# Causal attention in a decoder layer: query tiles of odd number with their quarters reversed, masked quarter products left out of every diagonal block, and the softmax sums' reciprocals turned on VectorE

## The chip, the cores and the metric

The kernel runs as one program on one core of a Trainium2 chip. The metric is the time of one execution on the device, in microseconds (us). A core has five engines that run their own instruction lists and wait for each other by semaphores: TensorE (PE in the profile; PEld is its loading of weights), VectorE (DVE), ScalarE (ACT), GpSimd (POOL) and SyncE (SP), which here issues most of the DMA transfers.

## The reference

A decoder layer on x (2 x 1024 tokens x 256 channels) with a context of 2 x 77 tokens, all in float32:

```python
x = _layernorm(x + self_attention(x))       # causal, 16 heads of 64, rotary positions on q and k
x = _layernorm(x + cross_attention(x, ctx)) # 16 heads of 64, 77 keys
x = _layernorm(x + routed_ffn(x))           # half of the tokens, hidden width 1024, exact gelu
```

The change lies in the self-attention, which for each batch and head is:

```python
sim = einsum('bid,bjd->bij', rope(x @ Wq), rope(x @ Wk)) * 64**-0.5
sim = where(tril, sim, -inf)
out = einsum('bij,bjd->bid', softmax(sim), x @ Wv)
```

A query i has no product with keys j > i: their weights are zero after the softmax.

## The kernel before

Self-attention takes the first 555 us or so of the execution, cross-attention and the feed-forward network the rest. Heads are worked two at a time: a `Pair` is one batch and two heads (their 128 channels), 16 pairs in all. Tokens are cut into 8 tiles of 128, and each tile into 4 quarters of 32.

For a pair the steps are, with the letters that the hand-written order uses:

- `P`, `E`: q, k and v are projected on TensorE (L257, L292) and copied out of PSUM by ScalarE (L265, L301).
- `d`, `c`, `s`, `a`: rotary positions, for half of the tokens at a time (0 or 1) and for k and q in one 128x1024 instruction each: two DMAs swap neighbouring rows (`swap`), GpSimd multiplies by the cosine (`cosine`, L277) and the swapped copy by the sine (L280), and adds both into the tile `kq` (`rotated`, L284). VectorE does this for half 0 of pair 0.
- `S`, `T`, `X`: scores of query tiles in five groups, (3,1,0), (4,2), (5), (6), (7), on TensorE (L331), each for keys up to the query tile's own; VectorE adds the tile `fence`, which holds the causal mask for the diagonal block in its last 128 columns and zeros before them, and takes the least (L344); ScalarE takes the exponential and its sum over keys (L352).
- `R`: VectorE turns the weights within 32x32 squares (L361) into `p_t`. There the partitions of quarter r hold the queries of quarter r's squares with keys down the partitions, so the product with the values is made of small matmuls on 32 rows and 64 columns of TensorE: row group r for quarter r of the queries, column group j for the head.
- `V0` to `V7` (`output`, L399): V*n* takes key tile n, for each of its quarters k, each head j and each row group r one matmul into `po[r]`, over the queries of the same quarter r in all query tiles from n on: 256, 224, ... 32 columns. For n < 7 all of them are made, also those of the diagonal block whose quarter of keys lies wholly after the quarter of queries (k > r); their weights are zeros. For n = 7 those are left out.
- `O`: ScalarE copies the four `po` out, quarter r to columns r*32 and on of each tile (L413); for the last pair VectorE multiplies while it copies (L419).
- `Q`, `I`, `D`, `B`, `M`, `W`: the sums are turned by a TensorE transpose into a PSUM tile `pr` (`sums_row`, L369), VectorE takes the reciprocal, 16x128, (L373), one DMA writes it to DRAM, 16 rows of 512 bytes (`flat`), two DMAs read it back spread over 64 partitions each (`along`), GpSimd multiplies (L422), and a DMA stores the pair's output.
- `w`, `l`: the values go to DRAM and come back in four copies, one for each row group, two of them issued by ScalarE.

After the 16 pairs the outputs are projected tile by tile, 8 matmuls each (`Closing.project`, L466), and normed.

All engines of this part follow an order written by hand. The list `steps` gives one period, in which steps of different pairs are interleaved; on TensorE it reads: S0 V0 V1 S1 V2 V3 V4 S2 V5 V6 V7 S3 Q Pk1 Pv0 S4 Pq1 Pq0 Pk0 Pv4. `opening` and `ending` give the first and the last pairs one by one. The DMAs of SP leave in the same order (`begin`), and the first of them after V1 and after V7 waits for that step's last matmul (`gate`). A PSUM ring of four buffers serves projections, `pr` and the four `po` in turn. The list `pieces` says, for each pair, how many matmuls are cut into smaller ones (`split`), which adds instructions.

The biases b2 and the router's row w_r of the feed-forward network are loaded early, after the stores of pairs 3 and 4.

Of the kernel before, what the change touches and what calls it, by code (L numbers as in the profile page):

```python
# [22 lines left out]
NT = T // P  # L23
# [11 lines left out]
def decoder_layer(  # L35
# [45 lines left out]
    causal = const.tile([P, P], F32)  # L81
    make_causal_mask(nc, causal, MASKED)
# [37 lines left out]
    b2 = const.tile([P, C], F32)  # L120
    b_r = const.tile([P, 1], F32)
    b1 = const.tile([P, NF], F32)
    w_r = const.tile([P, C], F32)
# [11 lines left out]
    with (  # L135
# [9 lines left out]
        fence = s1.tile([P, T], F32, name="fence")  # L145
        G.memset(fence[:, : T - P], 0.0)
        G.tensor_copy(fence[:, T - P :], causal)
        wo = s1.tile([P, NP, C], F32, name="wo")

        p_t = s1.tile([P, (NT + 1) * NT, P], F32, name="pT")  # L150
        attn_d = [dram.tile([NP, P, T], F32, tag="attn", name="attn_d") for _ in range(B)]
# [3 lines left out]
        def load(t, src):  # L155
            return lambda: nc.sync.dma_start(t, src)


        def load_next(h):
            if h == 0:  # L160
# [10 lines left out]
            3: [load(b2, L0_ffn_b2.partition_broadcast(P)), load(b_r, L0_ffn_b_r.partition_broadcast(P))],  # L171
            4: [
                load(w_r, L0_ffn_w_r.rearrange("c o -> (o c)").partition_broadcast(P)),
# [60 lines left out]

        class Pair:
# [39 lines left out]

            def cosine(self, n, E=G):
                E.tensor_tensor(self.kq[:, :, n * NB : (n + 1) * NB], self.raw[n], self.twice(cos, n), ALU.mult)  # L277
# [4 lines left out]
            def rotated(self, n, E=G):  # L282
                dst = self.kq[:, :, n * NB : (n + 1) * NB]
                E.tensor_tensor(dst, dst, self.turned[n], ALU.add)  # L284
# [54 lines left out]
            def least(self, g, j):  # L339
# [3 lines left out]
                for i, (t, span) in enumerate(self.spans[g]):  # L343
                    V.tensor_tensor_reduce(  # L344
                        p[:, span], self.ps[j][:, span], fence[:, T - (t + 1) * P :],
# [21 lines left out]
            def sums_row(self):  # L367
                self.pr = ring.tile([2 * NT, P], F32, tag="t", name="pr_sums")
                TE.transpose(self.pr, self.sums.rearrange("p j t -> p (j t)"), ident)  # L369

            def inverse(self):
                self.inv = small.tile([2 * NT, P], F32, tag="inv", name="inv", bufs=2)
                V.reciprocal(self.inv, self.pr)  # L373

            def flat(self):
                self.inv_d = dram.tile([2, NT * P], F32, tag="inv", name="inv_d")
                begin(self.inv_d.rearrange("j (t q) -> (j t) q", q=P), self.inv)
# [10 lines left out]
            def output(self, n):  # L388
                if n == 0:
                    self.po = [ring.tile([P, NT, R32], F32, tag="t", name="po_self") for _ in range(4)]  # L390
                for k in range(4):
                    for j in range(2):
                        first = (NT * n + n, NT * (n + 1) + n)[j]
                        step = (1, NT)[j]
                        last = first + (NT - 1 - n) * step + 1

# [861 lines left out]
```

## Time and profile before

| | |
|---|---|
| median of 3 runs | 796.13 us (793.79 to 797.62) |
| the profiled execution | 793.43 us |
| its span in the profile | 791.7 us, granted TensorE clock 0.997 |
| PE busy | 765.8 us, 97% of the span |
| PEld busy | 611.0 us, 77% |
| DVE busy | 556.8 us, 70% |
| ACT busy | 388.6 us, 49% |
| POOL busy | 369.4 us, 47% |

The profile is one execution. Its time as a run is 793.43 us; the span of its instructions is 1.7 us shorter. A group of the profile is given as line, engine, operation, written tile <- read tiles, shape and count, then busy time and mean duration, then the idle time of the engine just before those instructions and what ended it. "issue" there is idle time for which the profile shows nothing that was waited for. The chain of waits is followed backwards from the last instruction; each piece of it has its start, its length and its line. One pair's period in the middle of the self-attention is about 30 us long.

### The profile page before, as it was taken

The page shows a single profiled execution, that of the slowest core. Times are in us where ns is not written, and L with a number is a line of the kernel's source. Part 1 is how long each engine was busy: PE and PEld are TensorE (multiplying, and loading weights), DVE is VectorE, ACT ScalarE, POOL GpSimd, SP SyncE. Part 2 cuts the span into 40 slices and gives each one's busy share as a digit, 9 for nine tenths or more (in the row PEclk, how much of TensorE's full clock was granted, in tenths as well). Part 3 has the DMA queues.
Part 4 walks back from the last instruction along what each step waited for, and adds up shares of the span by engine and source line. Part 5 has one row for each costly group of instructions (what it writes and reads, how often), then busy time and mean ns, then how long its engine had stood idle before and what let it go on. Part 6 is the DMA issues. An engine that isn't in the chain of part 4 may idle for free.

```text
span 791.7 us, 26856 instructions
## 1 busy us (share of the span) xinstructions
PE 765.8 (97%) x11320; PEld 611.0 (77%) x11320; DVE 556.8 (70%) x1295; ACT 388.6 (49%) x1249; POOL 369.4 (47%) x264
## 2 busy tenths in 40 slices
PE   8998999999999999999999998989999999999996
PEld 5565788888888788888887877678967888777755
DVE  2578679769669669677787787915576678758773
ACT  2555456556566466554555554400565666552130
POOL 3633554554554554573654744124023332371665
PEclk9999999999999999999999999999999999999998
DMA  5456377477477476576573655766069888861131
GB/s 199 129 154 178 117 220 191 168 205 188 141 198 196 150 235 180 164 207 179 165 209 104 193 150 175 176 189 224 2 185 246 210 196 216 200 159 54 54 107 53
DMA packets 141412, 131.96 MB, mean 167 GB/s; under 512 B 79554, under 2 KB 117996, under 8 KB 141292
## 3 DMA queue, kind: packets, MB, share of 16 engines
q1 hardware_dynamic: 133132, 100.09, 46.5%
q10 hardware_dynamic: 6624, 25.96, 11.0%
q0 software_dynamic: 1536, 4.20, 1.5%
q8 instruction: 89, 1.46, 0.8%
q14 instruction: 31, 0.25, 0.1%
HBM read 81.68 MB, written 31.76 MB: 143 GB/s over the span
## 4 chain that ended last, share of the span: by engine, by line
PE 76%; DVE 8%; POOL 7%; issue 4%; DMA 2%; SPq 1%; ACT 1%; POOLq 0%; DVEq 0%; ACTq 0%
PE po_self L399 18%; PE ps_scores L331 16%; PE pp_kq L257 13%; PE pp_v L292 7%; PE po_proj L466 6%; PE po_cross L1044 4%; PE ps_cross L974 4%; PE pp_h L907 2%; POOL e_all L1002 2%; POOL comp L842 2%; PE po_ffn L922 2%; DVE reach L812 2%; DVE pT L361 1%; DMA turned<-raw 1%; DVE p L344 1%
## 5 line engine op out<-in xcount | busy, mean ns | idle before, releaser
L352 ACT ACTIVATE p<-p,neg 128x768 f32<-128x768 f32 (+7 forms) x256 | 196.3, 768 | 162.1 <-DVE neg L344 160.1
L344 DVE CUSTOM_DVE_ANT_0 p<-ps_scores,fence 128x512 f32<-128x512 f32 (+7 forms) x256 | 179.4, 750 | 103.4 <-PE ps_scores L331 103.0
L361 DVE STREAM_TRANSPOSE pT<-p 128x512 f32<-128x512 f32 (+7 forms) x256 | 175.7, 740 | 6.2 <-PE po_self L399 3.0
L399 PE MATMUL po_self<-pT,v 32*64 32x256 f32 (+6 forms) x7808 | 156.7, 295 | 11.4 <-issue 8.7
L399 PEld LDWEIGHTS po_self<-pT,v 32*64 32x64 f32 x7808 | 136.9, 130 | 35.6 <-issue 24.9
L331 PE MATMUL ps_scores<-kq 64*128 64x256 f32 (+3 forms) x1060 | 149.7, 411 | 1.5 <-POOL kq L284 0.8
L331 PEld LDWEIGHTS ps_scores<-kq 64*128 64x128 f32 x1060 | 94.4, 186 | 42.0 <-issue 27.1
L257 PE MATMUL pp_kq<-xT,w_pair 128*128 128x256 f32 (+2 forms) x524 | 118.6, 379 | 1.1 <-ACT xT L192 0.7
L280 POOL TENSOR_TENSOR turned<-turned,sin 128x1024 f32<-128x1024 f32 x31 | 73.3, 2363 | 94.4 <-DMA turned<-raw 81.5
L277 POOL TENSOR_TENSOR kq<-raw,cos 128x1024 f32<-128x1024 f32 x31 | 73.6, 2374 | 85.5 <-ACT raw L265 85.5
L257 PEld LDWEIGHTS pp_kq<-xT,w_pair 128*128 128x128 f32 x524 | 88.3, 190 | 23.9 <-issue 11.2
L993 ACT ACTIVATE e_all<-ps_cross,top 128x77 f32<-128x77 f32 x256 | 79.1, 340 | 53.2 <-DVE top L985 51.2
L1002 POOL TENSOR_TENSOR e_all<-e_all,inv 128x616 f32<-128x616 f32 x32 | 38.8, 1217 | 91.1 <-DVE inv L1000 91.0
L109 POOL TENSOR_TENSOR rs<-ve,neg_half 128x1 f32<-128x1 f32 x48 | 26.8, 561 | 107.9 <-DVE ve L107 107.7
L284 POOL TENSOR_TENSOR kq<-kq,turned 128x1024 f32<-128x1024 f32 x31 | 73.6, 2373 | 1.4
L1044 PE MATMUL po_cross<-packed,pT 128*128 128x256 f32 (+1 forms) x320 | 72.3, 380 | 0.3 <-DMA packed<-vo_d 0.3
L974 PE MATMUL ps_cross<-wqk,x1T 128*128 128x308 f32 x256 | 69.9, 425 | 0.3 <-ACT e_all L993 0.3
L1044 PEld LDWEIGHTS po_cross<-packed,pT 128*128 128x128 f32 (+1 forms) x320 | 60.0, 190 | 9.4 <-issue 0.7
L292 PEld LDWEIGHTS pp_v<-w_pair,xT 128*128 128x128 f32 x512 | 61.1, 192 | 4.0 <-issue 2.5
L292 PE MATMUL pp_v<-w_pair,xT 128*128 128x128 f32 x512 | 62.2, 275 | 0.0
L974 PEld LDWEIGHTS ps_cross<-wqk,x1T 128*128 128x128 f32 x256 | 47.2, 190 | 17.5 <-ACT e_all L993 1.4
L993 ACT ACTIVATION_READ_ACCUMULATOR e_all<-ps_cross,top 128x1 f32 x256 | 56.6, 221 | 0.0
(128 smaller groups left out, 787.2 us busy)
## 6 DMA issues: line engine op xcount, KB each, us to landing
turned<-raw SPq DMA_DIRECT2D x64, 256.0 KB, 5.0
v<-v_d ACTq DMA_DIRECT2D x32, 512.0 KB, 10.1
v<-v_d SPq DMA_DIRECT2D x32, 512.0 KB, 11.1
part_d<-part ACTq DMA_DIRECT2D x14, 640.0 KB, 4.4
pT<-part_d SPq DMA_DIRECT2D x56, 160.0 KB, 4.1
v_d<-v SPq DMA_DIRECT2D x16, 512.0 KB, 4.8
over<-inv_d SPq DMA_DIRECT2D x32, 256.0 KB, 4.7
attn_d<-out_pair SPq DMA_DIRECT2D x14, 512.0 KB, 4.2
```

Source lines behind the costliest of these rows:

```text
L257: TE.matmul(pp[:, cols], self.w[:, c, "kq".index(of), :], x_ts[self.b, n][:, c, cols], start=(c == 0), stop=(c == NC - 1),)
L277: E.tensor_tensor(self.kq[:, :, n * NB : (n + 1) * NB], self.raw[n], self.twice(cos, n), ALU.mult)
L284: E.tensor_tensor(dst, dst, self.turned[n], ALU.add)
L292: TE.matmul(pv[:, i, :], x_ts[self.b, 2 * n // NT][:, c, toks], self.w[:, c, 2, :], start=(c == 0), stop=(c == NC - 1),)
L331: TE.matmul(self.ps[j][:, cols], self.kq[rows, 1, t * P : (t + 1) * P], self.kq[rows, 0, cols.start - at : cols.stop - at], start=True, st ...
L344: V.tensor_tensor_reduce(p[:, span], self.ps[j][:, span], fence[:, T - (t + 1) * P :], -SCALE, -MASKED, ALU.add, ALU.min, neg[:, i : i + 1],)
L352: A.activation(p[:, span], p[:, span], AF.Exp, bias=neg[:, i : i + 1], scale=-1.0, accum_out=self.sums[:, j, t : t + 1],)
L361: V.transpose(p_t[:, first : first + t * step + 1 : step, :], self.p[g, j][:, span].rearrange("p (n k) -> p n k", k=P),)
L399: ins = TE.matmul(self.po[r][j * D : (j + 1) * D, n:, :], self.v4[rows, NT * k + n, j * D : (j + 1) * D], p_t[rows, first:last:step, k * R ...
L974: TE.matmul(ps[:, g, : Q * S], self.x_t[:, c, :], wqk[:, c, self.b, h : h + Q, :].rearrange("p h s -> p (h s)"), start=(c == 0), stop=(c = ...
L993: A.activation(self.e[:, hh * HH + h, :], sc[:, g, q, :], AF.Exp, bias=top[:, g, q : q + 1], accum_out=sums[:, h : h + 1],)
L1044: TE.matmul(po, self.p_t[:w, k, :], of[:w, k, :], start=(k == 0), stop=(k == NK - 1))
```

## The change

- The q half of `kq` is written with a new order of columns: in query tiles of odd number the four quarters stand in reverse order. Row group r then holds quarter r of even tiles and quarter 3-r of odd ones. `cosine` and `rotated` therefore become three instructions each: k, the even tiles of q, the odd tiles of q.
- A second fence holds the mask for the odd tiles' order of rows.
- `output` takes key tiles in twos. For each (key tile a, key quarter k) a row group whose quarter of queries in tile a lies wholly before the keys begins at tile a+1, so its matmul is 32 columns narrower (for a = 7 it is left out). The number of matmuls of a pair stays 244. Steps V0 to V7 keep their places in the order, but an even step now holds (m,0), (m+1,0), (m,1), (m+1,3) and the odd one (m,2), (m+1,2), (m,3), (m+1,1), with m the even key tile.
- The copies out of `po` put the quarters back.
- `sums_row` no longer uses TensorE and PSUM: VectorE takes the reciprocal of the sums as they lie (128x16, into a 128x32 tile), and `inverse` turns that tile within 32x32 squares on VectorE. `flat` becomes four DMAs, each of 16 partitions with 128 bytes.
- b2 and w_r are loaded at the start of the cross-attention, in a pool there.

```diff
-    causal = const.tile([P, P], F32)
-    make_causal_mask(nc, causal, MASKED)
-    b2 = const.tile([P, C], F32)
-    w_r = const.tile([P, C], F32)
...
-        fence = s1.tile([P, T], F32, name="fence")
-        G.memset(fence[:, : T - P], 0.0)
-        G.tensor_copy(fence[:, T - P :], causal)
+        fences = [s1.tile([P, T], F32, name=f"fence_{i}") for i in range(2)]
+        make_causal_mask(nc, fences[0][:, T - P :], MASKED)
+        G.memset(fences[0][:, : T - P], 0.0)
+        G.memset(fences[1], 0.0)
+        for r in range(4):
+            rows = fences[1][r * R32 : (r + 1) * R32, T - P :]
+            G.affine_select(
+                out=rows, in_=rows, compare_op=ALU.is_ge, fill=MASKED, base=(3 - r) * R32,
+                pattern=[[-1, P]], channel_multiplier=1,
+            )
...
+        invs = [s1.tile([P, R32], F32, name=f"inv_{i}") for i in range(2)]
+        for t in invs:
+            G.memset(t, 1.0)
...
-            3: [load(b2, L0_ffn_b2.partition_broadcast(P)), load(b_r, L0_ffn_b_r.partition_broadcast(P))],
+            3: [load(b_r, L0_ffn_b_r.partition_broadcast(P))],
             4: [
-                load(w_r, L0_ffn_w_r.rearrange("c o -> (o c)").partition_broadcast(P)),
...
+        def blocks(t):
+            return t.rearrange("p (t two r q) -> p t two r q", two=2, r=4, q=R32)
+        def tiles_of(t, odd):
+            return t if odd is None else blocks(t)[:, :, odd, :, :]
+        def turned_rows(t, r):
+            return t.rearrange("p t q -> p (t q)").rearrange("p (t b q) -> p t b q", b=8, q=R32)[:, :, r : 8 - r : 7 - 2 * r, :]
...
+            def parts(self, n):
+                k, q = (self.kq[:, i, n * NB : (n + 1) * NB] for i in range(2))
+                return [(k, 0, None)] + [(blocks(q)[:, :, i, :: 1 - 2 * i, :], 1, i) for i in range(2)]
             def cosine(self, n, E=G):
-                E.tensor_tensor(self.kq[:, :, n * NB : (n + 1) * NB], self.raw[n], self.twice(cos, n), ALU.mult)
+                for dst, i, odd in self.parts(n):
+                    E.tensor_tensor(
+                        dst, tiles_of(self.raw[n][:, i, :], odd), tiles_of(cos[:, n * NB : (n + 1) * NB], odd), ALU.mult
+                    )
             def rotated(self, n, E=G):
-                dst = self.kq[:, :, n * NB : (n + 1) * NB]
-                E.tensor_tensor(dst, dst, self.turned[n], ALU.add)
+                for dst, i, odd in self.parts(n):
+                    E.tensor_tensor(dst, dst, tiles_of(self.turned[n][:, i, :], odd), ALU.add)
...
-                        p[:, span], self.ps[j][:, span], fence[:, T - (t + 1) * P :],
+                        p[:, span], self.ps[j][:, span], fences[t % 2][:, T - (t + 1) * P :],
...
             def sums_row(self):
-                self.pr = ring.tile([2 * NT, P], F32, tag="t", name="pr_sums")
-                TE.transpose(self.pr, self.sums.rearrange("p j t -> p (j t)"), ident)
+                V.reciprocal(invs[self.n % 2][:, : 2 * NT], self.sums.rearrange("p j t -> p (j t)"))
             def inverse(self):
-                self.inv = small.tile([2 * NT, P], F32, tag="inv", name="inv", bufs=2)
-                V.reciprocal(self.inv, self.pr)
+                self.inv = small.tile([P, R32], F32, tag="inv", name="inv", bufs=2)
+                V.transpose(self.inv, invs[self.n % 2])
             def flat(self):
                 self.inv_d = dram.tile([2, NT * P], F32, tag="inv", name="inv_d")
-                begin(self.inv_d.rearrange("j (t q) -> (j t) q", q=P), self.inv)
+                dst = self.inv_d.rearrange("j (t b q) -> (j t) b q", b=8, q=R32)
+                for r in range(4):
+                    begin(dst[:, r : 8 - r : 7 - 2 * r, :], self.inv[r * R32 : r * R32 + 2 * NT, :])
...
-                for k in range(4):
+                m = n - n % 2
+                for a, k in [((m, 0), (m + 1, 0), (m, 1), (m + 1, 3)), ((m, 2), (m + 1, 2), (m, 3), (m + 1, 1))][n % 2]:
                     for j in range(2):
-                        first = (NT * n + n, NT * (n + 1) + n)[j]
-                        step = (1, NT)[j]
-                        last = first + (NT - 1 - n) * step + 1
-
-                        for r in range(k if n == NT - 1 else 0, 4):
+                        for r in range(4):
+                            t = a if (r, 3 - r)[a % 2] >= k else a + 1
+                            if t == NT:
+                                continue
+                            first = (NT * a + t, NT * (t + 1) + a)[j]
+                            step = (1, NT)[j]
                             rows = slice(r * R32, (r + 1) * R32)
                             ins = TE.matmul(
-                                self.po[r][j * D : (j + 1) * D, n:, :],
-                                self.v4[rows, NT * k + n, j * D : (j + 1) * D],
-                                p_t[rows, first:last:step, k * R32 : (k + 1) * R32],
-                                start=(n == 0 and k == 0), stop=(n == NT - 1 and k == r),
+                                self.po[r][j * D : (j + 1) * D, t:, :],
+                                self.v4[rows, NT * k + a, j * D : (j + 1) * D],
+                                p_t[rows, first : first + (NT - 1 - t) * step + 1 : step, k * R32 : (k + 1) * R32],
+                                start=(a == 0 and k == 0), stop=(m == NT - 2 and (a, k) == ((NT - 1, 1), (NT - 2, 3))[r == 3]),
                             )
...
-                A.copy(self.out[:, :, r * R32 : (r + 1) * R32], self.po[r])
+                A.copy(turned_rows(self.out, r), self.po[r].rearrange("p (t two) q -> p t two q", two=2))
...
+    b2 = c1.tile([P, C], F32, name="b2")
+    w_r = c1.tile([P, C], F32, name="w_r")
+    nc.sync.dma_start(w_r, L0_ffn_w_r.rearrange("c o -> (o c)").partition_broadcast(P))
+    nc.sync.dma_start(b2, L0_ffn_b2.partition_broadcast(P))
```

## The prediction

> **What bounds the kernel now.** First the page: busy shares, then the chain that ended last.
>
> ```profile
> span 791.7 us, 26856 instructions
> PE 76%; DVE 8%; POOL 7%; issue 4%; DMA 2%; SPq 1%; ACT 1%; POOLq 0%; DVEq 0%; ACTq 0%
> ...
> L399 PE MATMUL po_self<-pT,v 32*64 32x256 f32 (+6 forms) x7808 | 156.7, 295 | 11.4 <-issue 8.7
> L399 PEld LDWEIGHTS po_self<-pT,v 32*64 32x64 f32 x7808 | 136.9, 130 | 35.6 <-issue 24.9
> ```
>
> TensorE ends the execution, and L399, the line that is narrowed, is its largest part. Shares are averages, so I took the chain in order of time. One pair, the seventh:
>
> ```profile
> 229.46 1.72 PE ps_scores L331 x16
> 231.17 3.42 PE po_self L399 x128
> 234.60 1.93 PE ps_scores L331 x12
> 236.53 3.80 PE po_self L399 x192
> 240.33 1.49 PE ps_scores L331 x8
> 241.82 2.29 PE po_self L399 x126
> 244.11 1.72 PE ps_scores L331 x16
> 245.83 0.21 PE pr_sums L369
> ```
>
> Piece follows piece without a gap: from about 80 to 476 us (pairs 1 to 13) nothing but TensorE is on the path. VectorE is busy 22.64 of the 30.23 us of this period, GpSimd 16.80. What TensorE saves here is saved, until another wait appears. A stage view says which stretches can shrink: V0 and V1 take 3.43 us for 128 records, V2 to V4 3.80 for 192, V5 to V7 2.29 for 168.
>
> The third view, TensorE's own row by time, shows the one cost in L399 that is not matmul work (the eighth pair):
>
> ```profile
> 270.85 1.15 PE L399 MATMUL po_self<-pT,v 32*64 32x96 f32 x73
> 272.95 1.36 PE L399 MATMUL po_self<-pT,v 32*64 32x64 f32 x95 [0.95 <-issue]
> ```
>
> A stop of 0.95 us with nothing waited for. The queue of instruction packets explains it: 89 packets of 16 KB for some 22,900 instructions of TensorE, so 256 each, and the stops come where the count of instructions passes one remainder by 256, 2.4 to 2.9 us after a packet began to move. In pairs 2 to 13 they add up to about 4.7 us.
>
> **The change, part by part.** The sum is made against the profiled execution, 793.43 us; the median is 796.13, 2.7 above it, and I carry the difference over.
>
> *Narrower matmuls.* The records of V0 start in bursts of eight, one for each 32x64 tile of the array, 216 ns apart at 256 columns; then 189 at 224, 162 at 192, 135, 109, 82 at 96: 27 ns for 32 columns. A matmul has two records (7808 for 16 pairs of 244). In two steps of V, three times in turn some row groups and then the others are 32 columns narrower, so each row group loses 3 x 2 x 27 = 0.16 us. This is worth something only if a row group can run ahead of the rest. The records say yes: when the last pair's first four matmuls start alone at 509.95, the second record of the first comes 267 ns after its first, and the first records of the three others have started in between, out of the program's order.
>
> V0 and V1: -0.16. V2 to V4: -0.16 for key tiles 2 and 3, -0.16 because V4 now holds narrower work (870 to 710 ns), and V5 keeps its 0.66. V6 and V7: their bursts are already at 57 ns, near eight starts of 6.7 ns, so nothing. That is 0.48 us for a pair, 6.2 for the 13 pairs on the pure chain. Pair 0 stands between instruction stops and pair 15's V6 waits 2.57 us for instructions: 0.2 each. Pair 14 isn't TensorE's: 0. Sum -6.6; bounds 0 (no running ahead) and 16 x 0.64 = -10.2 (V6 and V7 gain too).
>
> The Trainium skill, "TensorE: Matmul & The Clock Gate", part 3, "The mechanism", says that matmuls start and end strictly in the program's order. By that rule a step lasts as long as its widest row group, no step is narrow in all four, and this term would be 0. The starts at 509.95 contradict it, so the sum goes by the trace.
>
> *No pr_sums.* From the last score to the next projection the switch costs 93 ns beyond the stream, with pr_sums between 209: -0.116 us, 14 times on the path, -1.6. Bounds 0 and 16 x 0.21 = -3.4.
>
> *Instruction stops.* The number of instructions stays, less two or three for each pair, so the packet boundaries move later by 3 instructions at pair 1 and some 30 at pair 13; `pieces` is unchanged. The stop in V6 follows S2 by a fixed time and moves with it. The one in V4 comes sooner by what V2 and V3 save: half of the pairs have margin there, half have none (their stops are 0 to 0.55). I take +0.12 for each of 13 pairs, +1.5. Bounds: -4.7 (all stops vanish) and +6.2 (all of the gain is waited away).
>
> *GpSimd.* A 128x1024 becomes 128x512 and two of 128x256.
>
> ```profile
> L284 POOL TENSOR_TENSOR kq<-kq,turned 128x1024 f32<-128x1024 f32 x31 | 73.6, 2373 | 1.4
> L459 POOL TENSOR_TENSOR xb<-x,bo 128x256 f32<-128x256 f32 x16 | 11.0, 699 | 0.0
> ...
> 290.38 2.39 POOL L284 TENSOR_TENSOR kq<-kq,turned 128x1024 f32<-128x1024 f32 x1
> 293.99 2.00 PE L331 MATMUL ps_scores<-kq 64*128 64x256 f32 x16
> ```
>
> By these rows 512 columns take 1257 ns and the three 2655, 0.28 more, for `cosine` and `rotated` each: 1.1 us for a pair, on an engine that idles 13. The closest reader is S1, which waits for half 1's `rotated`: it ends at 292.77, S1 starts at 293.99, 1.2 us later. S1 will come 0.16 earlier, and in the built program it waits for the first two parts only (1957 ns), so the cover of the odd part is S2, 5 us on. Cost 0. No row shows runs of 32 backwards; if they doubled a part (1400), S1's two would end 0.28 later, still covered. On VectorE (pair 0) the parts cost 0.3 more each; `rotated` ends at 16.77 and S0 starts at 19.09: 0.
>
> *VectorE.* The reciprocal of 16x128 takes 933 ns and of 128x8 191; so 128x16 some 240, and the 32-column turn some 171 (270 at 128, 1.03 ns a column): 0.41 for 0.93. Hidden in the middle; at the end it is on the chain:
>
> ```profile
> 506.13 0.86 DVE inv L373
> 506.99 0.97 DVE pT L361
> 507.96 0.83 DVE inv L373
> 508.79 2.23 DVE pT L361 x2
> ```
>
> Both stand before the last pair's V0: -0.9. Bounds 0 and -1.7. The fences' extra work on GpSimd (some 2.5 us) is done by 7 us, and VectorE's first read is at 21: 0.
>
> *SP.* `flat` issues four DMAs for one, +1.2 us at the 0.33 to 0.54 us of its rows. In the middle SP idles from 287.3 until V1 opens the next DMA at 294, and `along` comes after that: 0, though the two added waits on the value copies hold up the weights for three pairs later and the store, which nobody needs soon. At the end there is no cover:
>
> ```profile
> 507.02 0.33 SPq L208 DMA_DIRECT2D inv_d<-inv  x1
> 511.79 1.58 SPq L208 DMA_DIRECT2D over<-inv_d  x2
> ...
> 514.10 0.49 SPq L208 DMA_DIRECT2D inv_d<-inv  x1
> 520.13 1.09 SPq L208 DMA_DIRECT2D over<-inv_d  x2
> ```
>
> `along` waits for the write to land (4.8 and 6.0 us), and pair 15's stands behind pair 14's: 2 x 1.2 = 2.4 us later. VectorE multiplies at 526.28 to 527.70, and TensorE uses the result at 529.45: 1.75 us of cover, which TensorE's earlier V7 uses up. I take +1.5; bounds 0 and +4. The loads of b2 and w_r wait for exponentials of the last pairs and fall into SP's idle time from 540 to 577.7: 0.
>
> Sum: -6.6 - 1.6 + 1.5 - 0.9 + 1.5 = -6.1. 793.43 becomes 787.3, the median 790.0.
>
> **Rivals.** What this measurement can tell from no change is 0.5%, 4.0 us.
>
> *The instructions don't come faster.* Stops take the place of the gain. For it: half of the pairs already stop in V, and 256 instructions pass there in 3.4 to 4 us. Against it: a stop moves with S2, and pairs such as the seventh have none. At +6.2 instead of +1.5 the sum is -1.4: 794.7.
>
> *Row groups march in step.* First term 0, no added stops: -1.6 - 0.9 + 1.5 = -1.0: 795.1. Against it: the records at 509.95.
>
> *Backward runs of 32 are dear on GpSimd* (the other side). S1 starts late once its two parts pass 2.37 + 0.84 + 0.2 = 3.4 us, so once a 256-column part takes 2.1 us, three times the 699 ns row. At five times, 3.5 us, S1 is 1.35 late in 13 pairs, +17.5, and the sum +11: 807. It decides from about 2.9 us a part, where the sum passes 4. Against it: the normalising product on 128x616 with a repeated operand costs less per column than the plain one (1217 ns).
>
> *More than forecast:* V6 and V7 gain and stops vanish: -12, 784.
>
> **How the numbers follow.** Forecast 0.64, more 0.06, instructions 0.14, in step 0.06, GpSimd or another slower case 0.10. The forecast's own range, stops and end taken at their bounds one at a time, is 785 to 793; a tenth of it falls short of 0.5%. Faster 0.70, same 0.20, slower 0.10. For eight in ten the range runs from 785 to 797, over both cases without a change.
>
> **What would show it.** V0-V1 near 3.27 us and V2-V4 near 3.25 in a pair without a stop, V5-V7 still 2.29; matmul records of L399 unchanged at 7808; no pr_sums; stops in L399 in more pairs but not longer than 1 us; GpSimd's even part done before S1; `along` of pair 15 later after its write. Wrong it would be if V0-V1 stays at 3.43, if score matmuls wait for kq, or if the po_proj after V7 waits several us for out_pair.

## The result, and the profile after

The changed kernel took 820.82 us (median of 4 runs, 819.41 to 825.33); the kernel before took 795.63 beside it. The ratio is 1.0326, with a 95% interval of 1.0279 to 1.0373. The forecast was 790.0 with a range of 785 to 797: wrong in size and in sign. The profiled execution after took 820.90 us, its span 819.1, 27.4 longer than the span before.

First the page of the kernel after: the span, the chain's shares, and the two groups of the narrowed line (the last number of a group is the engine's idle time just before its instructions, and what ended it).

```profile
span 819.1 us, 27080 instructions
...
PE 80%; DVE 6%; issue 6%; POOL 5%; DMA 2%; ACT 1%; POOLq 0%; ACTq 0%; SPq 0%; DVEq 0%
...
L426 PE MATMUL po_self<-pT,v 32*64 32x224 f32 (+7 forms) x7808 | 154.9, 293 | 32.5 <-issue 30.7
L426 PEld LDWEIGHTS po_self<-pT,v 32*64 32x64 f32 x7808 | 138.7, 134 | 56.4 <-issue 49.7
```

L426 is the old L399. Its busy time fell a little, from 156.7 to 154.9, but TensorE stood still before it for 32.5 us, not 11.4, and "issue" says that nothing the profile shows was waited for. The chain in order of time shows where, in pair 7 (start, length, what):

```profile
266.50 3.27 PE po_self L426 x116
269.76 1.93 PE ps_scores L355 x12
271.69 2.83 PE po_self L426 x124
274.52 2.34 issue
276.87 0.94 PE po_self L426 x29
277.81 2.86 PE ps_scores L355 x8
280.67 2.17 PE po_self L426 x114
282.85 1.72 PE ps_scores L355 x16
```

V0 and V1 take 3.27 us, exactly the forecast. Then, inside V4, TensorE stops for 2.34 us. This is an instruction stop, of the kind that the prediction knew, but it is there in every pair from 2 to 13, 0.72 to 2.69 us long. After it the eight score matmuls, 1.49 us in other pairs, take 2.86. The same stretch by windows shows why (stretch, its length, busy time of PE, PEld, DVE, ACT and POOL with counts, granted TensorE clock, DMA share, GB/s):

```profile
271.62:274.53 2.91, 2.90 (x155) 2.73 (x154) 2.81 (x9) 0.66 (x1) 2.03 (x3) 1.00 0.96 276
274.53:276.87 2.34, 0.00 (x1) 0.00 (x0) 2.02 (x6) 2.27 (x8) 1.19 (x1) 1.00 0.14 32
276.87:277.74 0.87, 0.87 (x39) 0.75 (x38) 0.00 (x0) 0.00 (x0) 0.69 (x1) 0.70 0.00 0
277.74:280.60 2.86, 2.86 (x11) 1.18 (x8) 0.00 (x0) 0.00 (x0) 1.66 (x1) 0.50 0.03 9
```

Two things are to be seen. The DMA engines are 96% busy just ahead of the stop, and the clock granted to TensorE is halved after it.

I added up TensorE's records of both profiles by line, each piece counted to the start of the next. The matmuls with the values take 19.4 us more: 21.4 more of stops, 2.0 less of all else. The same score, projection and output-projection matmuls take 3.1, 1.2 and 3.2 us more; the granted clock is 0.5 to 0.7 for some microseconds after five of the stops, and its mean is 0.982 against 0.997. The transposes of the sums save 2.0. That is 24.9 of the 27.4 us; 1.7 more lie in the feed-forward network's first product, and the rest is in pieces below 1 us. Scores run for 10.3 us at half clock, output projections for 4.5 and the first product for 3.4; no projection of q and k does. Their 1.2 us are mostly the first projection of a pair, which takes 0.10 us longer where it now follows the scores directly.

### The profile page after: what moved, and what is told of

Same layout as the page of the kernel before. It is cut to its first block, busy times and chain, and to the rows that moved or that the text cites. A ratio compares the mean times of both kernels' runs of the same rounds, so it can differ in the third digit from the quotient of the medians.

```text
span 819.1 us, 27080 instructions
## 1 busy us (share of the span) xinstructions
PE 771.7 (94%) x11304; PEld 617.5 (75%) x11304; DVE 547.2 (67%) x1315; ACT 390.1 (48%) x1249; POOL 388.4 (47%) x394
## 4 chain that ended last, share of the span: by engine, by line
PE 80%; DVE 6%; issue 6%; POOL 5%; DMA 2%; ACT 1%; POOLq 0%; ACTq 0%; SPq 0%; DVEq 0%
PE po_self L426 18%; PE ps_scores L355 17%; PE pp_kq L273 14%; PE pp_v L316 7%; PE po_proj L495 6%; PE ps_cross L1007 4%; PE po_cross L1077 4%; PE pp_h L940 3%; POOL e_all L1035 2%; POOL comp L875 2%; PE po_ffn L955 2%; DVE reach L845 1%; DMA v<-v_d 1%; DVE part L1042 1%; DVE pT L385 1%
## 5 line engine op out<-in xcount | busy, mean ns | idle before, releaser
L426 PE MATMUL po_self<-pT,v 32*64 32x224 f32 (+7 forms) x7808 | 154.9, 293 | 32.5 <-issue 30.7
L426 PEld LDWEIGHTS po_self<-pT,v 32*64 32x64 f32 x7808 | 138.7, 134 | 56.4 <-issue 49.7
L355 PE MATMUL ps_scores<-kq 64*128 64x256 f32 (+3 forms) x1060 | 153.0, 421 | 1.3 <-DVE pT L385 1.3
L299 POOL TENSOR_TENSOR kq<-raw,cos 128x256 f32<-128x256 f32 (+1 forms) x93 | 82.3, 915 | 101.6 <-ACT raw L281 101.6
L308 POOL TENSOR_TENSOR kq<-kq,turned 128x256 f32<-128x256 f32 (+1 forms) x93 | 82.3, 915 | 1.4
```

The costliest lines, as they stand in the source:

```text
L299: E.tensor_tensor(dst, tiles_of(self.raw[n][:, i, :], odd), tiles_of(cos[:, n * NB : (n + 1) * NB], odd), ALU.mult)
L308: E.tensor_tensor(dst, dst, tiles_of(self.turned[n][:, i, :], odd), ALU.add)
L355: TE.matmul(self.ps[j][:, cols], self.kq[rows, 1, t * P : (t + 1) * P], self.kq[rows, 0, cols.start - at : cols.stop - at], start=True, st ...
L426: ins = TE.matmul(self.po[r][j * D : (j + 1) * D, t:, :], self.v4[rows, NT * k + a, j * D : (j + 1) * D], p_t[rows, first : first + (NT - ...
```

## The experiments

The DMAs that load the swapped rows (`turned`) and the spread reciprocals (`over`) wait for V1's last matmul. Their packets start 1.4 us after V1's end and keep the DMA engines busy until 6 to 7 us after it. Times are counted here from the start of S1, which is 0.07 us ahead of V1's modelled end in most pairs and up to 0.7 us behind it where S1 waits; so those packets start about 1.5 us after S1's start. For each pair I took from the trace where the boundary of 256 TensorE instructions falls within V2 (the stops stand exactly 256 instructions later, in V4), and when the packet that starts as TensorE gets there (the "request") begins to move. Pairs 2 to 13 (the stops in sums over these pairs):

```
kernel               boundary in V2   request after S1's start  stops, us: V2-V4  V5-V7   ratio to before
                     (instructions)   (us)
before               27 to 40          1.06 to 2.85                  0.9    3.1
after                34 to 61          2.87 to 4.84                 22.1    3.0    1.0326
retuned              26 to 34          1.47 to 4.87                  9.1    6.4    1.0055
shifted              27 to 65          2.35 to 4.68                 16.9    4.6    1.0260
threeparts           27 to 40          1.02 to 2.67                  0.7    4.5    1.0005
retuned_wide         26 to 34          1.05 to 4.26                  6.3    3.8    1.0036
recip                34 to 62          2.21 to 4.58                 18.9    5.7    1.0392
gate4                34 to 61          2.61 to 3.55                  9.6    7.1    1.0089
gate4_before         27 to 40          1.04 to 2.06                  0.0    0.6    0.9914
retuned_flat         26 to 34          1.23 to 2.98                  2.7    2.9    1.0082
gate4_retuned        26 to 34          1.19 to 3.43                  4.0    2.2    0.9907
gate4_retuned_flat   26 to 34          1.10 to 2.73                  0.7    0.3    0.9961
gate4_retuned_wide   26 to 34          1.11 to 3.76                  2.9    0.6    0.9930
gate4_shifted        27 to 65          1.49 to 3.33                  4.8    6.8    1.0084
gate4_late           26 to 34          1.14 to 2.04                  0.03   1.6    0.9818
gate4_late_wide      26 to 34          1.14 to 2.01                  0.0    0.2    0.9883
```

The stops are those of one profiled execution, the ratios are of several. Ratios are compared rather than times, since the kernel before had medians of 795.6 to 801.5 us beside the different sets.

### Is it the boundary, GpSimd, or the narrow steps?

Three theories were on record. P: the boundary lies too late. G: GpSimd's three parts release S1 later. N: the narrower steps pass 256 instructions too quickly for any packet.

`retuned`, the kernel after with other numbers in `pieces`:

```diff
-        pieces = [2, 1, 13, 13, 11, 10, 11, 12, 13, 12, 8, 9, 8, 8, 9, 0]
+        pieces = [2, 1, 14, 13, 12, 11, 10, 12, 13, 12, 9, 9, 8, 9, 9, 1]
```

> The kernel after, with six numbers of pieces changed, so that the boundaries of 256 TensorE instructions lie 26 to 34 instructions into V2 in pairs 2 to 13, as before (27 to 40), and not 34 to 62. Theory P (place of the boundary): the packet is asked for when the queue enters the block, in the kernel after too late to slip in ahead of the transfers that V1's end releases. Then the stops in V2 to V4 of pairs 2 to 13 fall from 22.0 us to under 5 and the time is 786 to 794 us. Theory G (GpSimd's three parts end later, S1 is released later, the queue can't run ahead): only pairs 10 to 13 gain, where the parts end 2.6 us before S1, 7 us in all: 811 to 815. Theory N (the narrower steps pass 256 instructions too quickly for any packet): stops remain in all pairs, 815 or more.

Measured: 806.83 us, 1.0055 (1.0019 to 1.0092). Four fifths of the loss is gone, with the narrow steps and GpSimd's parts as they were, so N falls. (Seven numbers of `pieces` differ.) But 9.1 us of stops are left in V2 to V4, where P expected under 5, and the time misses P's 786 to 794.

`shifted`, the kernel before, its `pieces` changed the other way:

```diff
-        pieces = [2, 1, 13, 13, 11, 10, 11, 12, 13, 12, 8, 9, 8, 8, 9, 0]
+        pieces = [2, 1, 13, 13, 10, 10, 10, 12, 13, 12, 7, 9, 8, 7, 9, 0]
```

> The kernel before, with pieces changed the other way: in pairs 4 to 13 the boundary lies 46 to 66 instructions into V2, as in the kernel after. Nothing else differs. Theory P: stops of 1 to 2.7 us in V4 of these ten pairs, 12 to 24 us in all, time 808 to 822. Theories G and N: 794 to 800, since GpSimd's instructions and the steps' widths are those of before.

Measured: 822.12 us, 1.0260 (1.0211 to 1.0310). The narrowed line's group in this kernel:

```profile
L399 PE MATMUL po_self<-pT,v 32*64 32x256 f32 (+6 forms) x7808 | 163.8, 302 | 32.2 <-issue 29.9 <-DVE pT L361 1.9
```

Idle 32.2 us where the kernel before has 11.4, and nothing of the change is in it: a few matmuls were left uncut. P holds.

`threeparts`, the kernel before with GpSimd's instructions in three parts (`parts` gives k, the even tiles of q and the odd ones, in their old order of columns):

```diff
...
-                E.tensor_tensor(self.kq[:, :, n * NB : (n + 1) * NB], self.raw[n], self.twice(cos, n), ALU.mult)
+                for dst, i, of in self.parts(n):
+                    E.tensor_tensor(dst, of(self.raw[n][:, i, :]), of(cos[:, n * NB : (n + 1) * NB]), ALU.mult)
...
-                E.tensor_tensor(dst, dst, self.turned[n], ALU.add)
+                for dst, i, of in self.parts(n):
+                    E.tensor_tensor(dst, dst, of(self.turned[n][:, i, :]), ALU.add)
```

> The kernel before, with cosine and rotated made in three instructions each (k, even tiles of q, odd tiles of q) with the quarters left in order. Theory G: S1's release comes 0.3 to 0.6 us later against V1's end, packets are late in pairs 2 to 9, time 804 to 815. Theory P: the boundaries are where they were, time 794 to 800.

Measured: 801.00 us, 1.0005 (0.9966 to 1.0043). The parts cost nothing; G falls.

`retuned_wide`, the kernel `retuned` without the narrowing:

```diff
-                            t = a if (r, 3 - r)[a % 2] >= k else a + 1
+                            t = a if a < NT - 1 or (r, 3 - r)[a % 2] >= k else a + 1
```

> The kernel retuned, but with the masked products made again as wide as before in key tiles 0 to 6 (those of key tile 7 stay left out); the number of instructions is the same, so the boundaries stay. It gives the price of the narrower products by itself. If the row groups run ahead of each other as forecast: 3.43 us again for V0 and V1, 3.56 for V2 to V4, and 5 to 7 us more than retuned. If they march in step: the same as retuned within 2 us. Theory N: faster than retuned, since the wider steps leave the packets more time.

Measured: 802.68 us, 1.0036 (1.0004 to 1.0068), not told apart from `retuned`. The steps did take 3.43 us again for V0 and V1 and 3.47 for V2 to V4 in pairs without a stop, so the narrow matmuls are shorter, and the time doesn't show it. The cause was therefore still open in part.

### Which part of the change moves the boundary, and what delays the packet?

`recip`, the kernel before with the sums' reciprocals alone:

```diff
...
-                self.pr = ring.tile([2 * NT, P], F32, tag="t", name="pr_sums")
-                TE.transpose(self.pr, self.sums.rearrange("p j t -> p (j t)"), ident)
+                V.reciprocal(invs[self.n % 2][:, : 2 * NT], self.sums.rearrange("p j t -> p (j t)"))
...
-                V.reciprocal(self.inv, self.pr)
+                V.transpose(self.inv, invs[self.n % 2])
...
-                begin(self.inv_d.rearrange("j (t q) -> (j t) q", q=P), self.inv)
+                dst = self.inv_d.rearrange("j (t r q) -> (j t) r q", r=4, q=R32)
+                for r in range(4):
+                    begin(dst[:, r, :], self.inv[r * R32 : r * R32 + 2 * NT, :])
```

> The kernel before, with one part of the change alone: the reciprocals of the sums taken and turned by VectorE, with the four small DMAs, and no transpose on TensorE. Nothing is narrower and no column reversed. Without the transpose the boundaries lie 46 to 62 instructions into V2 from pair 4 on, as in the kernel after. Theory P: the stops of the kernel after come back, 14 to 22 us of them in V2 to V4 of pairs 2 to 13, time 812 to 825. Any theory that blames the narrower products, the order of the steps or the reversed columns: 794 to 801, 2 us gained for the transposes.

Measured: 827.58 us, 1.0392 (1.0325 to 1.0458).

```profile
L403 PE MATMUL po_self<-pT,v 32*64 32x256 f32 (+6 forms) x7808 | 162.2, 297 | 31.1 <-issue 29.6 <-DVE pT L364 1.1 <-DVE y L480 0.2
```

This is the whole loss, from a part that takes work off TensorE; that it is more than the loss of the whole change isn't shown, the intervals overlap. Without the transpose each pair has two or three TensorE instructions fewer, and over the pairs the boundaries drift from the places for which `pieces` had been chosen. The four small DMAs are in this kernel too, so it doesn't give the price of the count by itself; `shifted` does.

`gate4` leaves the boundaries of the kernel after and moves the transfers (d0 loads the swapped rows, B the spread reciprocals):

```diff
-            ("s1", 0), ("V0", -1), ("a1", 0), ("V1", -1), ("d0", 1), ("B", -2), ("S1", 0), ("V2", -1), ("T10", 0),
-            ("V3", -1), ("V4", -1), ("T11", 0), ("S2", 0), ("X00", 0), ("V5", -1), ("R00", 0), ("X01", 0), ("R01", 0),
+            ("s1", 0), ("V0", -1), ("a1", 0), ("V1", -1), ("S1", 0), ("V2", -1), ("T10", 0),
+            ("V3", -1), ("V4", -1), ("d0", 1), ("B", -2), ("T11", 0), ("S2", 0), ("X00", 0), ("V5", -1), ("R00", 0), ("X01", 0), ("R01", 0),
...
-                if n in (1, NT - 1) and self.n < len(keys) - 1:
+                if n in (4, NT - 1) and self.n < len(keys) - 1:
```

> The kernel after, its boundaries where they were, but the transfers that waited for V1's last matmul (the swapped rows and the spread reciprocals) now wait for V4's, in the period and in pairs 1 and 2 of the opening. Theory P says that it is the collision with these transfers that delays the packet: the request after V2's boundary then meets idle queues, the packet arrives 2.6 us after the request and the stops in V2 to V4 of pairs 2 to 13 fall from 22.0 us to under 5, time 786 to 798. If the place of the boundary does harm by itself (too little run-ahead, whatever the transfers do): stops of about 0.7 us remain in each pair, 8 us, 803 to 808. A new wait could come from GpSimd, which gets the swapped rows 6 us later: S0 of the next pair would then show waits for kq.

Measured: 805.46 us, 1.0089 (1.0058 to 1.0120). Stops of 0.26 to 1.23 us remain in V2 to V4 of every pair. So the collision is about half of it, and the place does harm by itself, the second case of the expectation.

In `opening` the same two steps move behind V4 in pairs 0 and 1 as well. `gate4_before` is this edit made to the kernel before.

> The kernel before with the same move of the transfers behind V4. Its boundaries let most packets slip in ahead of the transfers already, so 0 to 5 us can be gained (its stops in V5 to V7 may grow or go): 790 to 801. Theory P: with the transfers out of the way the narrower products of gate4 show their worth, gate4 is 4 to 8 us below this kernel. If they are worth nothing, the two are equal within 2 us.

Measured: 792.45 us, 0.9914 (0.9879 to 0.9950). No stop at all is left in V2 to V4. The chain of pair 7:

```profile
260.01 3.42 PE po_self L399 x128
263.44 1.93 PE ps_scores L331 x12
265.37 3.56 PE po_self L399 x183
268.92 1.49 PE ps_scores L331 x8
270.41 2.28 PE po_self L399 x127
```

The comparison with `gate4`, however, came out against the narrow products: `gate4` was slower, not 4 to 8 us faster.

`gate4_shifted` puts the two causes apart: `gate4_before` with the `pieces` of `shifted`.

> The kernel before with its transfers behind V4 and the pieces of shifted: boundaries 46 to 66 instructions into V2 from pair 4 on, no transfers running there, nothing of the change. Theory R: requests at 2.6 to 3.5 us after V1's end and not at 1.0 to 2.1, stops of 0.2 to 1.0 us in V2 to V4 of pairs 4 to 13, and as large ones in V5 to V7; 8 to 15 us above gate4_before, a ratio to the kernel before of 0.998 to 1.01. If the transfers alone did the harm: as gate4_before, 0.991.

Measured: 806.55 us, 1.0084 (1.0054 to 1.0115), 1.7% above `gate4_before`. Its chain in pair 8:

```profile
299.57 1.93 PE ps_scores L331 x16
301.51 3.02 PE po_self L399 x152
304.53 0.48 issue
305.01 0.91 PE po_self L399 x40
...
308.55 0.70 issue
```

So of the 2.6% in `shifted`, 1.7 points come from the place alone, and the transfers, in the place of before, add the rest (`gate4_before` is itself 0.9 points below before; from 0.9914 to 1.0260 there are 3.5 points, half from each). The requests of the kernels with no transfer in the way tell how: boundaries 26 to 40 instructions into V2 are requested 1.0 to 2.1 us after S1's start (`gate4_before`, `gate4_late` and its wide twin), boundaries 46 to 65 in at 2.85 to 3.33 (`gate4_shifted`, pairs 4 to 13). S1 stands between V1 and V2, in most pairs 24 instructions that take 1.93 us, 80 ns each, while instructions of V2 pass in some 10 ns. If the queue can be at most about 50 instructions ahead of the matmul at work, a boundary that lies 20 instructions later is entered when S1 has gone 20 of its instructions further: up to 1.6 us. This run-ahead is inferred from the requests' times; no view shows the queue itself.

### What was left

`retuned_flat`, the kernel `retuned` with the four small DMAs issued by ScalarE:

```diff
-                    begin(dst[:, r : 8 - r : 7 - 2 * r, :], self.inv[r * R32 : r * R32 + 2 * NT, :])
+                    nc.scalar.dma_start(dst[:, r : 8 - r : 7 - 2 * r, :], self.inv[r * R32 : r * R32 + 2 * NT, :])
```

> The kernel retuned, with the four small DMAs that write the reciprocals issued by ScalarE, so that SyncE's queue of loads and stores behind them is no later than before. In retuned the two largest stops, pairs 4 and 8 (2.1 and 2.9 us), stand where the transfers were still running at V1's end (from 0.5 us on and not from 1.5). Theory F (the four DMAs make SyncE's queue late, and its stores run into V1): the stops in V2 to V4 fall from 9.1 us to under 4, time 4 to 8 us below retuned. If the four DMAs are not to blame: as retuned within 2 us, or slower for the work on ScalarE.

Measured: 804.30 us, 1.0082 (1.0050 to 1.0114). In its profile the stops fell from 9.1 to 2.7 us, as theory F said; its time is that of `retuned`, where F expected 4 to 8 us less. Inconclusive by itself, but see the kernel with ScalarE's issues below.

`gate4_retuned` joins the edits of `gate4` and `retuned`, `gate4_retuned_wide` and `gate4_retuned_flat` add the ones shown above.

> The kernel gate4 with the pieces of retuned: transfers behind V4, boundaries 26 to 34 instructions into V2. Theory R (run-ahead: TensorE's queue enters the next block at most some 50 instructions ahead of the matmul at work; near S1, where 24 instructions take 2 us, a boundary 20 instructions later costs 1 to 1.7 us of the packet's lead): requests at 1.0 to 2.1 us after V1's end as in gate4_before, no stop over 0.3 us in V2 to V4 of pairs 2 to 13, and the stops of gate4 (9.6 us there, 7.5 us in V5 to V7) all but go: 14 us below gate4, a ratio to the kernel before of 0.975 to 0.988. If place and transfers do not explain the rest of the loss: a ratio over 0.995.

> The kernel gate4_retuned with the masked products of key tiles 0 to 6 as wide as before. With no stops in the way this is the price of the narrower products alone: 0.16 us in V0 and V1, 0.2 to 0.3 in V2 to V4 and 0.1 in V5 to V7 for each of 14 pairs, 5 to 7 us more than gate4_retuned. If the packets are still the limit, less than 2 us more, or fewer us than gate4_retuned.

> The same with the four small DMAs issued by ScalarE. Theory F: they make SyncE's queue late, in some pairs its stores run past V1; worth 1 to 3 us if packets still meet those stores, so a ratio of 0.972 to 0.985. Else as gate4_retuned.

Measured: 791.26 us, 0.9907 (0.9881 to 0.9932); wide 793.20, 0.9930 (0.9895 to 0.9966); with ScalarE's issues 795.81, 0.9961 (0.9929 to 0.9992). The first is 14 us below `gate4`, as expected, and now faster than before, though its ratio falls short of the 0.975 to 0.988 expected. The narrow products are worth some 2 us in it, which is within the noise, and the way over ScalarE costs more than it brings. Its profile, of the fastest of its ten executions, shows few stops but V0 and V1 stretched to 3.7 to 3.9 us in five pairs; why is not settled. It also shows one long wait, before V0 of pair 14:

```profile
470.85 4.35 ACTq L402 DMA_DIRECT2D inv_d<-inv  x3
475.25 1.15 ACT L376 ACTIVATE p<-p,neg 128x1024 f32<-128x1024 f32 x1 [4.48 <-DMA inv_d<-inv]
477.82 1.16 PE L426 MATMUL po_self<-pT,v 32*64 32x256 f32 x6 [4.81 <-DVE pT L385]
```

ScalarE's exponentials stand behind its issues of the small DMAs, and TensorE waits 4.81 us for what follows them. `retuned_flat` has the same wait, 4.86 us; `gate4_retuned` stands 0.58 us in V0 and V1 of that pair.

`gate4_retuned` still had four late pairs, 2, 3, 7 and 8. In these, the packet of the boundary before, that of V0, starts less than 0.7 us ahead of S1's start and not 1.1 to 2.3; so the request in V2 is late as well. SyncE's queue around pair 7 of the kernel after shows what is in its way:

```profile
257.09 4.65 SPq L213 DMA_DIRECT2D inv_d<-inv  x4
261.86 0.40 SPq L213 DMA_DIRECT2D w_pair<-in_L_attn_Wk_dram  x1
263.81 0.40 SPq L213 DMA_DIRECT2D w_pair<-in_L_attn_Wq_dram  x1
264.25 0.47 SPq L213 DMA_DIRECT2D w_pair<-in_L_attn_Wv_dram  x1
264.83 0.41 SPq L213 DMA_DIRECT2D attn_d<-out_pair  x1
```

The four small DMAs hold SyncE for 4.65 us (the one DMA of before took 0.53 in this pair), and the weights and the 512 KB store behind them leave so late that they run into V0 and V1 (266.4 to 269.7). `gate4_late` moves only their place in the list:

```diff
-            ("X30", 0), ("M", -2), ("R20", 0), ("Ek1", 1), ("d1", 1), ("R31", 0), ("Ev0", 2), ("D", -1), ("S4", 0),
-            ("R30", 0), ("Pq1", 2), ("L", 3), ("W", -2), ("A", 0), ("c1", 1), ("X21", 0), ("Pq0", 2), ("T41", 0),
+            ("X30", 0), ("M", -2), ("R20", 0), ("Ek1", 1), ("d1", 1), ("R31", 0), ("Ev0", 2), ("S4", 0),
+            ("R30", 0), ("Pq1", 2), ("L", 3), ("W", -2), ("D", -1), ("A", 0), ("c1", 1), ("X21", 0), ("Pq0", 2), ("T41", 0),
```

> The kernel gate4_retuned with the four small DMAs moved behind the next weights' loads and the store in SyncE's queue (step D behind W). In gate4_retuned these four take up to 4.6 us of SyncE's time ahead of the loads and the store; in pairs 2, 3, 7 and 8 the store's packets run on to V1's end, the packet of V0's boundary starts 0.04 to 0.64 us before V1's end and not 2.2, and the next one is late in its turn (requests at 2.7 to 3.4 us, stops of 0.7 to 1.4). Theory F: with the old order of loads and stores these requests come at 1.0 to 2.1 us again, no stop over 0.3 us in V2 to V4 of pairs 2 to 13, 2 to 6 us below gate4_retuned: a ratio to the kernel before of 0.983 to 0.988. If SyncE's order is not to blame: 0.990 to 0.993, as gate4_retuned.

> The same with the masked products of key tiles 0 to 6 as wide as before: the price of the narrower products where no packet is late. As forecast, 5 to 7 us above gate4_late, a ratio of 0.990 to 0.996. If the narrower products only let TensorE arrive at the next late packet or the next wait sooner: within 2 us of gate4_late.

Measured: 784.89 us, 0.9818 (0.9769 to 0.9866), and 790.89 us, 0.9883 (0.9837 to 0.9928) with the wide products, run beside each other. All requests come at 1.14 to 2.04 us, the stops in V2 to V4 are 0.03 us in all, and the narrow products are worth 6.0 us between the medians of six runs each (4.9 between their means, with some 2.8 of noise to either side). `gate4_late` beats the kernels before and after, and so do `gate4_before` and `gate4_retuned`. The group of `gate4_late`, for comparison with the 32.5 us after:

```profile
L426 PE MATMUL po_self<-pT,v 32*64 32x224 f32 (+7 forms) x7808 | 149.0, 288 | 5.2 <-issue 4.9
```

Its chain in pair 8 shows what is late next:

```profile
278.26 9.38 DMA turned<-raw
...
287.77 2.37 POOL turned L304
...
290.21 1.97 POOL kq L308 x2
...
292.23 2.07 PE ps_scores L355 x16
294.30 3.27 PE po_self L426 x146
297.57 1.49 PE ps_scores L355 x8
299.06 2.21 PE po_self L426 x111
```

S1 now waits for the first two parts of `rotated`: V0 and V1 with this wait take 4.22 us. S1 waits 0.53 us in each of pairs 3, 7 and 8; with V0 and V1 themselves longer there, pairs 3, 7, 8 and 9 lose 3.2 us in all up to S1's start. V2 to V4 take 3.27, V5 to V7 2.2.

## Why the prediction was wrong, point by point

**The step that failed: "Instruction stops", +1.5 with bounds of -4.7 and +6.2.** It counted correctly that the boundaries move later, by 3 instructions at pair 1 and some 30 at pair 13, and that `pieces` stays. But it let each stop keep its place and its packet its hour, and so added 0.12 us a pair. Measured: +21.4 us. Two things were missing. First, next to S1 a shift of 20 instructions makes the request over a microsecond later, not 20 times 10 ns (1.0 to 2.1 us became 2.85 to 3.33 with no transfer in the way); that the queue's run-ahead is the reason is inferred. Second, the request then falls behind the transfers that V1's end releases (2.6 to 3.6 us in `gate4`, 2.9 to 4.8 in the kernel after). The trace of before had both: requests at 1.06 to 1.49 us in five of the twelve pairs, just ahead of the packets of `turned` at 1.5, and at 1.85 to 2.85 in the others. The prediction also took 3.4 to 4 us for 256 instructions in V; from the boundary in V2 to the one in V4 its own trace has 2.33 to 2.50 us, hardly time enough for the 2.4 to 2.9 us that pass from a packet's start to TensorE's resumption. And the stops of before in pairs 2 to 13 are 4.0 us (0.9 and 3.1), not 4.7. The upper bound was no bound: "all of the gain is waited away" limits a stop to what was saved, while a late packet costs as long as it is late.

**Not in the sum at all: the clock.** After five of the stops, 2.1 to 2.7 us long, the granted clock fell, to a mean of 0.5 to 0.7 over five microseconds. Scores and output projections took 3.1 and 3.2 us more, and both ran partly at half clock.

**"SP": cost 0 in the middle.** Wrong, though hidden by the larger loss. The prediction asked whether anybody needs the delayed loads and the store soon. Nobody does; what counts is which of TensorE's packets they meet. Moving the four DMAs behind the loads and the store took 0.9 points off (0.9907 to 0.9818).

**"Narrower matmuls", -6.6.** Right where no packet is late: 6.0 us between `gate4_late_wide` and `gate4_late`. V0 and V1 went from 3.43 to 3.27 in every pair up to 13 of the kernel after, the matmul records stayed 7808, V2 to V4 went to 3.27 (3.25 was forecast). V5 to V7 gained 0.1, where nothing was forecast. The row groups do run ahead of each other. In the kernel after, all but 2.0 of it was lost again: V2 to V4 without their stop take 3.56 us there (pair 4: 4.28 with a stop of 0.72), not 3.27, some 0.3 us beside the stop's own length.

**"No pr_sums", -1.6.** Mis-sized. The transposes' stretches, 2.0 us in all, are gone, but the first projection after the scores is 0.10 us longer for it: in pairs 1 to 8 the time from the last score's start to the second projection's start went from about 0.428 us to 0.415. The prediction had measured the switch only up to the first projection's start. By this the term is worth some 0.2 us. Its real price was the instructions that it takes out of the count: `recip`, with the four DMAs in it, lost 3.9%.

**"GpSimd", 0.** Right in `threeparts` (1.0005) and in the kernel after, where the idle time ahead of the scores is 1.3 us and ended by VectorE. The two parts that S1 waits for take 1.97 us in `gate4_late` (1957 ns was forecast). But the cover of 1.2 us, read from one pair, isn't there in all. In the kernel before S1 waited 0.39 us for `kq` in pair 4, and its chain left TensorE there, though the prediction has nothing but TensorE on the path from 80 to 476 us:

```profile
160.29 8.82 DMA turned<-raw
...
171.68 2.39 POOL kq L284
174.12 2.06 PE ps_scores L331 x12
```

After, no pair waits so; in `gate4_late` three do.

**"VectorE", -0.9, and the chain D to B at the end, +1.5.** Not told apart in the kernel after, where the last pair's stop of 2.10 us covers them. In `gate4_late`, which has no such stop, the wait is there, 2.43 us, inside the bounds of 0 and 4:

```profile
516.98 4.49 PE L495 MATMUL po_proj<-wo,attnT 128*128 128x256 f32 x12 [2.43 <-DVE out_pair L445]
```

**The rivals.** "The instructions don't come faster" named the right cost at a quarter of its size, but let the stops eat the gain at most, and had neither the packets' hour nor the transfers in it; `shifted` has the stops with the steps as wide as before. "In step" and "backward runs dear" fell. The prediction's own test, "stops in more pairs but not longer than 1 us", failed in its second half, by stops of up to 2.69. Among the chances, if a tenth of the forecast falls short of 0.5%, "faster" adds up to 0.64 and not to 0.70.

The Trainium skill, "Runtime: NRT & Kernel Launch", section "Instruction fetch mechanics", says that instructions come in blocks of 256 and that passing from one to the next is mostly hidden. The first agrees with this trace; the second does not: 22.1 us of stops in twelve pairs.

## What to carry to other kernels

Where small matmuls pass 256 instructions in about the time that a packet of instructions needs to come (2.2 to 2.5 us against 2.4 to 2.9 from request to resumption here), the count of instructions is part of the schedule: any edit that adds or removes even two instructions a period has to be costed by where the boundaries fall, and by which transfers run when the next packet is asked for. Look in the trace at the packets of the instruction queue and at how near they already are to being late; a kernel whose requests lie within half a microsecond of a burst of transfers stands at an edge. What helped here was both: the burst and the queue ahead of it moved away from the instruction-hungry stretch, and the counts fitted (`gate4`, without the counts, stayed at 1.0089; `retuned`, without the move, at 1.0055).

## What the runs showed that was not expected

- A stop of TensorE of some 2 us can halve its clock. Of the stops over 0.9 us in the kernels `before`, `after`, `retuned`, `recip`, `shifted` and `gate4`, only one below 1.5 us was followed by a lower clock (1.17 us, in `shifted`); among those of 1.57 to 3.63 us some were (1.57, 1.94, 2.26) and some were not (1.82, 2.16, 2.57). The first five microseconds after such a stop had a mean clock of 0.50 to 0.69. The records of the granted clock show what divides them: in all sixteen traces every change of it falls on one grid of steps of 3.413 us. From full clock, every step in which TensorE was idle for more than 0.54 of the time was followed by half the clock, no step under 0.37 was, and between these both happened; so a stop that straddles two steps can pass (the 2.57 us of the kernel before is split so, with 0.44 of the first step idle). The Trainium skill, "TensorE: Matmul & The Clock Gate", Part 1, gives an idle window of about 3.4 us that runs freely; the grid agrees with such a window, but here a step idle by half, and at the least by 0.37, sufficed.
- The slow clock can outlast the stage. In the kernel after, the last pair's stop of 2.10 us was followed by output projections at half speed. The first twelve took 5.04 us, the later ones 2.75:

```profile
549.25 5.04 PE L495 MATMUL po_proj<-wo,attnT 128*128 128x256 f32 x12
...
558.44 2.75 PE L495 MATMUL po_proj<-wo,attnT 128*128 128x256 f32 x12
```

- The packet's own transfer (0.88 to 1.95 us for 16 KB) varied less than its start: behind the transfers it began up to 2.7 us after TensorE had entered the block (2.5 in the kernel after, the DMA engines 96% busy), and without them between 1.1 us before (`gate4_before`) and 1.2 us after that (`gate4`).
